# A list scheduler's priorities, a margin for transfers, and five tiles for rows of B, in a convolution, attention and selective-scan kernel

## The chip, the cores and the metric

The kernel runs on one core of one Trainium2 chip. A core has five engines with an instruction stream each: TensorE (PE, with its weight loads shown apart as PEld), VectorE (DVE), ScalarE (ACT), GpSimd (POOL) and SyncE (SP), which here issues the DMAs. The metric is the device time in microseconds; lower is better. All times are of fp32 work.

## The reference, cut to what matters

The input x has eight images of 56 x 56 tokens and 192 channels. Layer 0 adds to x an attention over a depthwise convolution of its group norm. Layer 1 adds a two-dimensional selective scan (SS2D), which is where most of the work lies:

```python
xz = einsum('bhwc,oc->bhwo', gn(x), in_proj_w)     # 192 -> 2 x 384
xa, z = split(xz)
xc = silu(depthwise_conv3x3(xa) + conv_b)
xs = [xc, xc transposed, and both reversed]         # 4 directions
dts, Bs, Cs = split(x_proj(xs))                     # 12, 16 and 16 rows
delta = softplus(dt_proj(dts) + bias)
for l in range(3136):                               # per direction
    h = exp(delta * A) * h + delta * B * u          # 384 channels x 16 states
    y[l] = sum over the 16 states of h * C
y = sum of the four directions (+ D * u)
out = x + out_proj(layernorm(y) * silu(z))
```

## The kernel before, in words

**Tiling.** A sequence of 3,136 tokens is cut into 7 chunks of T = 448 tokens. An image has 4 directions, so 28 chunks; the eight images have 224. Channels lie on the partitions, in 3 blocks j of 128. A chunk is scanned state by state, 16 states n, so there are 3,584 pairs (chunk i, state n). "Image" and "batch" mean the same below.

**Stages of the scan.** Each stage is a Python generator (lines 1044 to 1295):

- `prepared`: for each chunk, loads 12 delta rows (dts), C (ct_s) and the chunk of x (into du_s); PE projects the rows, and ACT and DVE make a softplus of them in the tile dl_s (L1066 to L1085, seven steps for each of three blocks); POOL then makes du_s = dl_s * x (L1089). dl_s and du_s have two tiles each.
- `row_loads`: for each state, broadcasts a row of B to 128 partitions (tile bb, 224 KB), and a row of C (cb) where POOL does the output.
- `inputs_made`: POOL makes h = du_s * bb, three blocks in one instruction (L1126). Tile h is taken from a ring of HBUFS tiles.
- `decays`: ACT makes da = exp(dl_s * A), a block at a time (L1140, two tiles).
- `scans`: DVE runs the recurrence in place in h (L1157). `carries`: DVE takes the last column as the start of the next chunk (newc, L1179).
- `turned`, `scaled`, `back`: PE transposes h (L1203, tile ht), ACT scales it by C (L1219, tile g), PE transposes it back and sums it over the states in PSUM (y, L1237; one y for the whole core).
- `by_pool`, `summed`: for 5 of the 16 states (3 in the last image), POOL multiplies h by C itself (L1256, L1260, tile yp) and PE adds the result to y (L1275).
- `skips` loads the chunk of x for the D term, and `evicted` adds y to the accumulator yacc on DVE (L1290, L1292).

Beside the scan of image b, `front` (group norms, convolutions, attention) and `x_proj` of image b + 1 are computed, and `finish` (layer norm, gate, output projection) of image b as its last direction ends.

**What sets the order.** None of this is written in the order in which it is issued. A list scheduler (class `Sched`) runs at build time. Every generator yields requests: an engine, an assumed cost, the cells that the step reads and those that it writes. `Sched.run` keeps a clock for each engine and takes, of all requests that can go, the one with the smallest t - rank, where t is the later of its inputs' and its engine's times. A rank of 0.4 thus lets a step be taken before another that could start up to 0.4 us sooner. The order found becomes the instruction order of each engine; on the chip the engines keep that order and wait on semaphores for the data. The ranks of the 13 scan stages are set where they are spawned (L1326): 0.30 for `prepared`, then 0.01 more for each, in the order `skips`, `row_loads`, `inputs_made`, `decays`, `scans`, `carries`, `turned`, `scaled`, `by_pool`, `back`, `summed`, `evicted` (0.42). `front` and `finish` have rank 0, and `URGENT` when they are behind their pace. For a DMA, the request has a fifth number: how long after its issue the data is assumed to be there.

```python
end = t + s.req[4] if len(s.req) > 4 else end + LATE[e]
```

Where the scheduler finds PE without work for over 0.45 us, it puts in fillers, matmuls of zeros (L1371)[...]. All DMAs go through SP's one queue, in the order found; a load that waits for its tile holds what stands behind it.

Of the kernel before, what the change touches and what calls it, by code (L numbers as in the profile page):

```python
# [21 lines left out]
T = 448  # L22
# [19 lines left out]
BY_POOL = (((2, 7), (12,)), ((2, 5), (8, 10), (13,)))  # L42
EPS = 1e-5
CAP = 60.0
HBUFS = 8
LEAD = 3


# [5 lines left out]
PE, ACT, DVE, POOL, SP = range(5)  # L54
LATE = (0.17, 0.08, 0.09, 0.06, 0.0)
HOP = 0.04
URGENT = 0.4


FILL = 64  # L60
# [103 lines left out]
class Sched:  # L164
# [37 lines left out]
    def give(self, s, t):  # L202

        e, cost, reads, writes = s.req[:4]
        end = t + cost
        self.at[e] = end
        self.used[e] += cost
        if s.group is not None and e == PE:
            self.spent[s.group] = self.spent.get(s.group, 0.0) + cost
        end = t + s.req[4] if len(s.req) > 4 else end + LATE[e]  # L210
        for c in reads:
            c.r = max(c.r, end)
        for c in writes:
            c.w = end
        s.end = max(s.end, end)
        self.resume(s)

    def run(self, until=None):
        while True:
# [20 lines left out]
            for s in self.stages:  # L240
# [3 lines left out]
                if s.group in self.limit:  # L244
# [4 lines left out]
                    if spent < must:  # L249
                        rank = URGENT  # L250
                e, _, reads, writes = s.req[:4]
# [21 lines left out]
def kernel(  # L273
# [93 lines left out]
    for nm, src in (("q", bn_q), ("kv", bn_kv)):  # L367
        p = load(f"bn{nm}", [CP, 4, NB], src.rearrange("v (b p) -> p v b", p=CP))
        s = const.tile([CP, NB], F32, name=f"bns{nm}")
        t = const.tile([CP, NB], F32, name=f"bnt{nm}")  # L370
# [30 lines left out]
    s3 = Rings(ctx.enter_context(tc.tile_pool(name="s3", bufs=3)), 3)  # L401
    sh = Rings(ctx.enter_context(tc.tile_pool(name="sh", bufs=HBUFS)), HBUFS)
    c1 = Rings(ctx.enter_context(tc.tile_pool(name="c1", bufs=1)), 1)
# [3 lines left out]
    sc = Sched()  # L407
# [57 lines left out]
    def dma(reads, writes, late, dst, src, after=()):  # L465
        yield SP, 0.07, reads, writes, late
        nc.sync.dma_start(dst, src)
        for t in after:
            t.free()
# [563 lines left out]
    for i in range(2):  # L1033
        t = keep.tile([128, T], F32, name=f"dts{i}")
# [70 lines left out]
    def row_loads():  # L1105
        for i, n in todo:
            b, k, c, _ = steps[i]
            yield lambda: i in chunks
            m = made[b]
            cols = slice(c * T, (c + 1) * T)  # L1110
            bb = yield s3("bb", [128, T])
            yield from dma([m["k_rows"][k, c]], bb.c, 3.2, bb.ap, m["rows"][k][R + n, cols].partition_broadcast(128))
            brow[i, n] = bb
            if n in by[i]:
                cbr = yield s2("cb", [128, T])
                yield from dma([m["k_rows"][k, c]], cbr.c, 3.2, cbr.ap,
                               m["rows"][k][R + NST + n, cols].partition_broadcast(128))
                crow[i, n] = cbr
# [178 lines left out]
    with tc.manual_schedule():  # L1297
        order = [(lay, c) for lay in range(2) for c in range(NCH)]

        with tc.tile_pool(name="p8", bufs=8, space=PSUM) as p8:  # L1300
            banks[0] = Ring(lambda: p8.tile([128, 512], F32, name="bank0"), 8)
            sc.spawn(front(0), 0.0, "front")
            sc.run()
            main = sc.spent.pop("front")
            sc.spawn(x_proj(0, order[:LEAD]), 0.0, "front")
            sc.run()
            each = sc.spent.pop("front") / LEAD

        with ExitStack() as es:
            py = es.enter_context(tc.tile_pool(name="py", bufs=1, space=PSUM))  # L1310
            pa = es.enter_context(tc.tile_pool(name="pa", bufs=2, space=PSUM))
            pb = [es.enter_context(tc.tile_pool(name=f"pb{i}", bufs=1, space=PSUM)) for i in range(3)]
            ybanks = py.tile([128, NJ, 512], F32, name="y")
            nc.vector.memset(ybanks, 0.0)
            ry = Ring(lambda: ybanks, 1)
            rda = Ring(lambda: pa.tile([128, 512], F32, name="da"), 2)
            three = [Tile(1) for _ in pb]

            def share(name, most):
                return Share(three, [lambda p=p: p.tile([128, 512], F32, name=name, tag="bank") for p in pb], most)  # L1320

            rht, rprep = share("ht", 2), share("prep", 1)
            banks[0] = share("bank1", 1)
            at["chunk"] = 0

            for rank, g in enumerate((prepared, skips, row_loads, inputs_made, decays, scans, carries, turned, scaled,  # L1326
                                      by_pool, back, summed, evicted)):
                sc.spawn(g(), 0.3 + 0.01 * rank, "scan")

            per = NDIR * NCH * NST  # L1330

            def ended(b):
                first = b * NDIR * NCH + (NDIR - 1) * NCH
                yield lambda: at["chunk"] >= first
                yield from finish(b, lambda c: lambda: at["chunk"] >= first + NCH - c, yread[b])

            def arounds():
                for b in range(nb):
                    yread[b] = {}
                    sc.spawn(ended(b), 0.0, "finish")  # L1340
                    if b > 0:
                        yield lambda: at["chunk"] >= b * NDIR * NCH
                    else:
                        yield from sc.join([sc.spawn(x_proj(0, order[LEAD:]), 0.0, "front")])
                    if b + 1 < nb:
                        yield from sc.join([sc.spawn(front(b + 1), 0.0, "front")])
                        yield from sc.join([sc.spawn(x_proj(b + 1, order), 0.0, "front")])

            def pace():

                b, slot = divmod(at["scan"], per)
                whole = main + len(order) * each
                lead = each * (len(order) - LEAD)
                before = b * whole + (lead if b else 0.0)
                here = whole + (0.0 if b else lead)
                late, share = (NDIR - 1) * NCH * NST, 0.87
                part = share * slot / late if slot < late else share + (1.0 - share) * (slot - late) / (per - 2 * NST - late)
                want = before + here * part
                return want + 12.0, want - 12.0

            def ending():
                done = sum(len(r) for r in yread.values())
                b, c = divmod(at["chunk"], NDIR * NCH)
                come = b * NCH + max(c - (NDIR - 1) * NCH, 0)
                return 1e9, 1e9 if done < come - 1 or done < b * NCH else 0.0

            def warm():

                while True:
                    yield PE, T_FILL, [], []  # L1370
                    nc.tensor.matmul(ybanks[:, 0, T:T + FILL], zeros, zeros[:, :FILL], start=False, stop=False)  # L1371

            def may():
                y = ys.get(at["y"])
                return y is not None and y["left"][0] > 0 and y["on"]

            at["y"] = -1
            filler = Stage(warm(), 0.0, 0.0, None)
            sc.resume(filler)
            sc.filler = filler, may  # L1380
            sc.limit["front"] = pace
            sc.limit["finish"] = ending
            sc.spawn(arounds(), 0.0)
            sc.run()
# [58 lines left out]
```

## Time and profile before

| | us |
|---|---|
| median of 3 runs (lowest, highest) | 18,865.54 (18,856.12, 18,895.47) |
| the profiled execution | 18,891.11 |
| its span, first to last instruction | 18,889.4 |
| busy: PE / DVE / ACT / POOL | 16,973.1 / 14,534.5 / 14,643.6 / 16,416.5 |
| granted TensorE clock, mean | 0.971 |
| DMA: share of 16 engines, rate | 32.2%, 93 GB/s |

The span covers all but 1.7 us of the profiled execution. Line numbers are those of the kernel before; in the changed kernel all lines after the constants are one higher. A group of instructions is shown as: line, engine, operation, tile written and tiles read, shapes, count, then busy us in all and mean ns of one, then the idle time of the engine just before them, with what ended most of it. The list of waits gives us in all, times, and the longest.

### The profile page before, as it was taken

To read this page: it belongs to the slowest core of one execution; us is meant where nothing else is said; L and a number is where in the kernel's file an instruction comes from. 1 tells how busy PE (TensorE), PEld (TensorE's weight loads), DVE (VectorE), ACT (ScalarE), POOL (GpSimd) and SP (SyncE) were. 2 spreads that over 40 slices of the span, in tenths; PEclk is the share of its full clock that TensorE was granted. 3 is DMA by queue.
4 is the path that set the end of the run, shared out by engine and by line. 5 is a ranking of instruction groups with operands and counts; after the bars stand their busy time and mean duration, and the time that the engine had idled before them with its cause. 6 is when DMAs were issued, how large, how long until landed. Compare 5 with 4: busy or idle time off the path is not lost. (4 is left out here: it accounts for less than half of the span.)

```text
span 18889.4 us, 274433 instructions
## 1 busy us (share of the span) xinstructions
PE 16973.1 (90%) x96640; PEld 11599.8 (61%) x96640; DVE 14534.5 (77%) x19156; ACT 14643.6 (78%) x26598; POOL 16416.5 (87%) x7528
## 2 busy tenths in 40 slices
PE   8789998999889998899898998889988899988888
PEld 4465566666666656665666655666556665666776
DVE  2387877887778777787777877778777788778887
ACT  2378877787777878778787887878778788888888
POOL 0388998899989999899998999989999899999997
PEclk9899999999999999999999999999999999999999
DMA  1332334323333333322333333332333333342222
GB/s 52 111 89 82 96 96 120 82 85 92 104 112 84 83 95 104 112 84 81 105 100 107 83 84 101 104 106 83 83 96 110 100 83 86 100 120 76 78 78 64
DMA packets 1128347, 1750.79 MB, mean 93 GB/s; under 512 B 168516, under 2 KB 1110840, under 8 KB 1123896
## 3 DMA queue, kind: packets, MB, share of 16 engines
q1 hardware_dynamic: 1126968, 1733.23, 32.2%
q8 instruction: 764, 12.52, 0.3%
q14 instruction: 615, 5.04, 0.1%
HBM read 1545.05 MB, written 187.74 MB: 92 GB/s over the span
## 5 line engine op out<-in xcount | busy, mean ns | idle before, releaser
L1157 DVE TENSOR_TENSOR_SCAN h<-da,newc,h 128x448 f32<-128x448 f32 x9216 | 10111.4, 1136 | 2166.1 <-ACT da L1140 1155.7
L1126 POOL TENSOR_TENSOR h<-du_s,bb 128x1344 f32<-128x1344 f32 x3584 | 10836.0, 3050 | 280.5 <-DMA bb<-rows 246.0
L1140 ACT ACTIVATE da<-dl_s,acoef 128x448 f32<-128x448 f32 x10752 | 6762.2, 636 | 1149.4 <-DVE h L1157 968.0
L1219 ACT ACTIVATE g<-ht,ct_s 112x384 f32<-112x384 f32 x10080 | 5663.7, 576 | 1776.0 <-PE ht L1203 1701.2
L1237 PE MATMUL y<-ident,g 112*128 112x112 f32 x30240 | 4742.3, 271 | 660.2 <-ACT g L1219 506.3
L1237 PEld LDWEIGHTS y<-ident,g 112*128 112x128 f32 x30240 | 3305.9, 143 | 3236.8 <-ACT g L1219 2466.3
L1203 PE MATMUL ht<-ident,h 128*112 128x128 f32 x30240 | 4935.7, 277 | 287.4 <-DVE h L1157 87.4
L1203 PEld LDWEIGHTS ht<-ident,h 128*112 128x112 f32 x30240 | 3481.3, 135 | 1064.4 <-issue 450.9
L1256 POOL TENSOR_TENSOR yp<-h,cb 128x448 f32<-128x448 f32 x1932 | 2147.0, 1143 | 454.8 <-PE y L1275 216.6
L1157 DVE TENSOR_TENSOR_SCAN h<-da,h 128x448 f32<-128x448 f32 x1536 | 1598.9, 1077 | 406.0 <-ACT da L1140 214.3
L1089 POOL TENSOR_TENSOR du_s<-dl_s,du_s 128x1344 f32<-128x1344 f32 x224 | 682.6, 3047 | 1338.5 <-DVE dl_s L1085 1300.8
L1256 POOL TENSOR_TENSOR h<-h,cb 128x448 f32<-128x448 f32 x1260 | 1399.1, 1141 | 291.3 <-issue 175.6
L1371 PE MATMUL y<-zeros 128*128 128x64 f32 x11944 | 1651.3, 272 | 0.0
L1371 PEld LDWEIGHTS y<-zeros 128*128 128x128 f32 x11944 | 1586.1, 198 | 48.6 <-issue 48.6
L1275 PE MATMUL y<-yp,ident 128*128 128x448 f32 x3864 | 1594.0, 547 | 5.1 <-POOL yp L1260 4.5
L453 PE MATMUL bank<-xa,dg 128*128 128x440 f32 (+2 forms) x3024 | 1318.4, 543 | 89.0 <-ACT g L1219 52.2
L1260 POOL TENSOR_TENSOR yp<-yp,h 128x1344 f32<-128x1344 f32 x420 | 1280.9, 3050 | 1.6
L757 PE MATMUL bank<-qT,kT 128*112 128x448 f32 x2352 | 1101.8, 559 | 83.8 <-ACT pT L707 47.2
L766 PE MATMUL bank<-pT,vt 112*128 112x448 f32 x2352 | 1002.1, 546 | 66.8 <-ACT pT L707 43.4
L1275 PEld LDWEIGHTS y<-yp,ident 128*128 128x128 f32 x3864 | 701.3, 193 | 551.6 <-issue 505.2
L453 PE MATMUL bank<-band,dgq 96*96 96x440 f32 (+3 forms) x2016 | 860.9, 544 | 54.4 <-ACT hq L583 29.9
L707 ACT ACTIVATE pT<-bank,nsh 112x448 f32<-112x448 f32 x1176 | 744.3, 635 | 172.9 <-PE bank L757 152.5
(152 smaller groups left out, 12958.1 us busy)
## 6 DMA issues: line engine op xcount, KB each, us to landing
bb<-rows SPq DMA_DIRECT2D x3584, 224.0 KB
cb<-rows SPq DMA_DIRECT2D x1064, 224.0 KB
xt<-x1d SPq DMA_DIRECT2D x224, 336.0 KB
du_s<-xch SPq DMA_DIRECT2D x112, 672.0 KB
du_s<-xcw SPq DMA_DIRECT2D x112, 672.0 KB
xch<-xv SPq DMA_DIRECT2D x24, 1568.0 KB
xcw<-xw SPq DMA_DIRECT2D x168, 224.0 KB
xs<-xch SPq DMA_DIRECT2D x56, 672.0 KB
```

The lines of the kernel that those rows point to most:

```text
L453: nc.tensor.matmul(out[:, o0:o1, a:b], lhs, img(lo, hi)[:, :, a + dx - 1:b + dx - 1], start=(t == TAPS[0]), stop=(t == TAPS[-1]))
L757: nc.tensor.matmul(ps.ap[:TP, :T], kts[h][:, kb * TP:(kb + 1) * TP], qh.ap, start=True, stop=True)
L1126: nc.gpsimd.tensor_tensor(h.ap, du.ap, bb.ap.unsqueeze(1).to_broadcast([128, NJ, T]), ALU.mult)
L1140: nc.scalar.activation(da.ap[:, :T], dl.ap[:, j], AF.Exp, scale=acoef[:, k * NJ + j, n:n + 1])
L1157: nc.vector.tensor_tensor_scan(h.ap[:, j, rev], da.ap[:, 0:T][:, rev], h.ap[:, j, rev], news[i - 1].ap[:, j, n:n + 1] if ci else 0.0, ALU. ...
L1203: nc.tensor.transpose(ht.ap[:TP, j * 128:(j + 1) * 128], h.ap[:, j, s * TP:(s + 1) * TP], ident)
L1219: nc.scalar.activation(g.ap, ht.ap[:TP, :DIN], AF.Copy, scale=ct.ap[:, s, n:n + 1])
L1237: nc.tensor.matmul(y["t"].ap[:, j, s * TP:(s + 1) * TP], g.ap[:, j * 128:(j + 1) * 128], ident[:TP, :TP], is_transpose=True, start=(n == 0 ...
L1256: nc.gpsimd.tensor_tensor(to.ap[:, j], h.ap[:, j], cbr.ap, ALU.mult)
L1260: nc.gpsimd.tensor_tensor(yp.ap, yp.ap, h.ap, ALU.add)
L1275: nc.tensor.matmul(y["t"].ap[:, j, :T], ident, yp.ap[:, j], start=False, stop=(y["left"][j] == 0))
L1371: nc.tensor.matmul(ybanks[:, 0, T:T + FILL], zeros, zeros[:, :FILL], start=False, stop=False)
```

## The change

It sets constants and ranks; no step of the computation is added or taken out.

- A DMA's data is assumed to be there `MARGIN` = 3 us later than before.
- `URGENT` goes from 0.4 to 0.9.
- Rows of B (bb) have five tiles instead of three; h has seven instead of eight. In bytes per partition of SBUF: 2 x 1,792 more, 5,376 less.
- The 13 stages get a rank each, by name.

```diff
-HBUFS = 8
+HBUFS = 7
...
-URGENT = 0.4
+MARGIN = 3.0
+URGENT = 0.9
...
-        end = t + s.req[4] if len(s.req) > 4 else end + LATE[e]
+        end = t + s.req[4] + MARGIN if len(s.req) > 4 else end + LATE[e]
...
-            bb = yield s3("bb", [128, T])
+            bb = yield s3("bb", [128, T], 5)
...
-            for rank, g in enumerate((prepared, skips, row_loads, inputs_made, decays, scans, carries, turned, scaled,
-                                      by_pool, back, summed, evicted)):
-                sc.spawn(g(), 0.3 + 0.01 * rank, "scan")
+            for g, rank in ((prepared, 0.3), (skips, 0.0), (row_loads, 0.25), (inputs_made, 0.0), (decays, 0.37),
+                            (scans, 0.16), (carries, 0.36), (turned, 0.37), (scaled, 0.38), (by_pool, 0.39),
+                            (back, 0.4), (summed, 0.0), (evicted, 0.71)):
+                sc.spawn(g(), rank, "scan")
```

## The prediction

> **What bounds the kernel now.** I read the page's busy shares first: five engines, none full, POOL the fullest of those with work of their own.
>
> ```profile
> PE 16973.1 (90%) x96640; PEld 11599.8 (61%) x96640; DVE 14534.5 (77%) x19156; ACT 14643.6 (78%) x26598; POOL 16416.5 (87%) x7528
> ```
>
> PE's 90% includes fillers. The costliest groups show how much, and what POOL does:
>
> ```profile
> L1126 POOL TENSOR_TENSOR h<-du_s,bb 128x1344 f32<-128x1344 f32 x3584 | 10836.0, 3050 | 280.5 <-DMA bb<-rows 246.0
> ...
> L1256 POOL TENSOR_TENSOR yp<-h,cb 128x448 f32<-128x448 f32 x1932 | 2147.0, 1143 | 454.8 <-PE y L1275 216.6
> ...
> L1089 POOL TENSOR_TENSOR du_s<-dl_s,du_s 128x1344 f32<-128x1344 f32 x224 | 682.6, 3047 | 1338.5 <-DVE dl_s L1085 1300.8
> L1256 POOL TENSOR_TENSOR h<-h,cb 128x448 f32<-128x448 f32 x1260 | 1399.1, 1141 | 291.3 <-issue 175.6
> L1371 PE MATMUL y<-zeros 128*128 128x64 f32 x11944 | 1651.3, 272 | 0.0
> ```
>
> Fillers (L1371) are 1651 us, so PE's own work is 15,322 us, under POOL's 16,416. POOL starts at 783.6 us (the first du_s) and could not end before 783.6 + 16,416 = 17,200 us. It loses 18,889.4 - 17,200 = 1,690 us: the last column gives du_s 1,338 less the start, L1126 280, L1256 455 + 291. POOL's list of waits separates the start:
>
> ```profile
> POOL du_s L1089 <- DVE dl_s L1085: 1300.8, 78, 729.9
> POOL h L1126 <- DMA bb<-rows: 246.0, 74, 9.7
> POOL yp L1256 <- PE y L1275: 216.6, 55, 12.9
> ...
> POOL h L1256 <- DVE newc L1179: 93.0, 36, 10.1
> ...
> POOL du_s L1089 <- DVE newc L1179: 37.4, 13, 6.4
> ```
>
> 729.9 us is the prologue, so du_s waits 1,338.5 - 729.9 = 609 us in the scan, always at the seam of two chunks. The timeline of POOL and of DVE at one seam:
>
> ```profile
> 8031.45 3.05 POOL L1126 TENSOR_TENSOR h<-du_s,bb 128x1344 f32<-128x1344 f32 x1
> 8041.89 3.04 POOL L1089 TENSOR_TENSOR du_s<-dl_s,du_s 128x1344 f32<-128x1344 f32 x1 [7.39 <-DVE dl_s L1085]
> 8045.01 12.06 POOL L1126 TENSOR_TENSOR h<-du_s,bb 128x1344 f32<-128x1344 f32 x4
> ...
> 8041.20 0.61 DVE L1085 TENSOR_TENSOR dl_s<-prep,dl_s 128x448 f32<-128x448 f32 x1
> 8041.73 0.61 DVE L595 TENSOR_REDUCE qm<-qe 128x1 f32<-128x448 f32 x1
> 8048.09 3.48 DVE L1157 TENSOR_TENSOR_SCAN h<-da,newc,h 128x448 f32<-128x448 f32 x3 [5.75 <-POOL h L1126]
> ```
>
> The delta of the new chunk (dl_s) is finished at 8,041.8 us; POOL has stood 7.39 us, makes du_s, then the first h, and DVE has stood 5.75 us when its scan starts. Taking the start of every state's first scan from the trace, over the seven batches with front work a state follows the last one after 4.74 us on average inside a chunk and after 9.38 us at a seam. The seam is not idle everywhere: PE is busy there with its own work 8.64 of the 9.38 us. Last, the batches, cut at their first scans (columns: busy us of PE, PEld, DVE, ACT, POOL):
>
> ```profile
> 7679.00:9980.00 2301.00, 2088.13 (x11792) 1414.47 (x11790) 1810.38 (x2386) 1815.64 (x3296) 2085.67 (x965) 0.97 0.33 96
> ...
> 16875.00:18889.00 2014.00, 1763.72 (x12360) 1400.34 (x12359) 1701.65 (x2186) 1738.70 (x3225) 1812.60 (x763) 0.96 0.27 78
> ```
>
> In a batch with front work PE (fillers in) and POOL are both busy 2,086 to 2,088 of 2,301 us. That pair is what limits the gain.
>
> **What the Trainium skill says.** "Perfetto Trace Analysis", Tensor Engine Instruction: ACT, DVE and GpSimd are strict first-in first-out. The trace agrees: nothing of POOL's passes the du_s that stands 7.39 us. "GPSIMD Engine Reference", 2.1 Instruction dispatch: a two-input body has a floor near 2.5 cycles per element; at its 1.2 GHz an estimate of 2.8 us for 1,344 elements, beside 3.05 us measured, so order can't shorten POOL's work, only its waits. "DMA: Bandwidth & Descriptors", Anatomy of one DMA: about 2.0 us fixed plus bytes / 436 GB/s (for GpSimd's path), and waits are held by the issuing sequencer. An estimate of 2.5 us for a 224 KB row of B; in this trace the product starts 3.8 us after the issue at the earliest, 9.4 us in the median.
>
> **The change part by part.** The programs of both kernels have the same instructions on DVE (19,158), ACT, POOL and SP (7,013, so no DMA more or less); PE has 340 fillers more (5,972 to 6,312). All else is order.
>
> *Delta earlier (ranks of prepared, scans, inputs_made).* Before, stage prepared (0.30) stood under scans (0.35) and inputs_made (0.33); now it stands over both (0.16 and 0). In the order of the built programs, du_s came after all 16 products of the chunk before in each of 224 chunks; now it comes 5.1 states earlier on average (2 at least). On DVE the last dl_s moves from 1.6 states ahead of its chunk's first scan to 7.6. Its loads move too: the 12 delta rows (dts) are issued on SP 18 rows of B ahead of the chunk's own instead of 16, its xs rows 9 instead of 10; both still lie ahead of need. So the 609 us of du_s waits should fall to some 40: -569. Ends: 0 if dl_s is late again, -609.
>
> *Rows of B (five tiles, MARGIN).* A tile's next load waits on SP for the product that frees it; with three tiles there are two products, about 9.4 us, between issue and use, with five four. Behind a waiting row on SP stand stores and loads of the front, which gain likewise. 246 us of waits to some 60: -186. Ends: 0, -246. MARGIN puts every user of a transfer 3 us later in the order; on the chip it waits only if the order has nothing else for it.
>
> *POOL's shares of y (by_pool, summed).* L1256 waits 746 us. In the orders POOL has made 2.2 states beyond the one it multiplies before, 2.9 after, so scan and carry are done more often when POOL comes to it; against it, summed falls from 0.41 to 0, which frees yp later (216.6 us of the 746). I take a third off, -250; ends +200, -500.
>
> *Seven h tiles.* L1126 waits 280 us in all, 246 for rows of B; so at most 35 us for a free h with eight. Taken as nothing, since products lie only 0.2 to 6.8 us ahead of their scans on average (hidden by that slack); up to +100 if POOL, no longer stopped at seams, runs into the seventh tile.
>
> *Urgent front (0.4 to 0.9), back, evicted.* Front work that is behind its pace now goes ahead of everything. PE's runs of front matmuls between scan matmuls grow longer: 288 of over 3 us instead of 113 (at 0.81 us per 448 columns, from three of L1275 in 2.42 us). The work is the same; ACT waits for ht longer in a run and less elsewhere. Zero, ends -100 and +790 (below).
>
> *Fillers.* 340 x (1,651.3 / 5,972 = 0.277 us) = 94 us on PE, 289 of them in the last batch, where PE has 2,014 - 1,764 = 250 us idle. Hidden; +94 if not.
>
> Sum on POOL: -569 - 186 - 250 = -1,005 us, or 125 us a batch. That would put a 2,297 us batch at 2,172 with PE and POOL both at 96%. Two in-order engines that wait for each other don't both get there; I give back 40% (waits of PE on g, of POOL on h) and take -600: batches near 2,222, both engines at 94%. 18,889 - 600 = 18,289 us for the profiled span. That execution took 18,891.1 us, the median of the runs is 18,865.5, so x 0.9986: 18,265 us.
>
> **Rivals.**
> (a) *PE is the wall.* For: at the seam PE was busy 8.64 of 9.38 us, and in batches 1 to 6 the fillers stay at 664 to 673 each (664 to 674 before), so the order leaves PE as much to wait as ever. Against: fillers aren't work, and PE idles 213 us a batch besides. Then two thirds of the gain of seams and rows go (755 / 3 = 250): about 18,600.
> (b) *Nothing is given back*: all 1,005 us: about 17,860. For: POOL's lead is larger everywhere. Against: both engines at 96%.
> (c) *Front bursts starve the scan*, slower. Place: PE, where ht and y stand behind a run of front matmuls, ACT waits for ht (1,701 us already), h tiles stay taken, with one fewer. Price: 175 more runs of some 4.5 us, 790 us if each stops the scan for its length: 18,865 - 600 + 790 = 19,055. It decides from 600 / 175 = 3.4 us lost in each. Against: POOL and DVE have slack of up to 6.8 us, and the total of front work is unchanged.
> (d) *The seam only moves*: delta is early but decays or y's single bank (evicted) hold the first scan: no change, 18,865.
>
> **How the numbers follow.** Forecast 0.60 (18,000 to 18,500), (a) 0.17, (b) 0.12, (c) 0.08, (d) 0.03. The range runs from (b) to the upper part of (a): 17,850 to 18,780, leaving out some 0.06 below and 0.13 above. Faster by over 0.2% (38 us, about what a measurement here tells from none) 0.88: forecast, (b) and nearly all of (a); within 0.2% 0.03; slower 0.09.
>
> **What would show it.** Right: L1089's wait under 770 us in all with the prologue, L1126's for bb under 100, seams near 5.5 us, POOL at 89 to 91% of the span, batches near 2,222. Wrong: seams as before, or ACT's wait for ht and PE's for g up by hundreds of us; a new POOL wait on h behind PE ht would point to the seventh tile; a last batch longer than 2,014 us to the fillers.

## The result, and the profile after

The changed kernel takes 18,645.61 us (median of 4 runs, 18,636.89 to 18,648.41), beside 18,874.99 us for the kernel before. The ratio is 0.9874, 95% interval 0.986 to 0.9888: faster by 1.3%, or 229 us. The forecast was 18,265 us, 3.2% faster. The time lies in the stated range, and the direction was right, but the gain is less than half of what was forecast.

The groups that the prediction was built on, in the page of the changed kernel (idle time before the group stands last):

```profile
L1127 POOL TENSOR_TENSOR h<-du_s,bb 128x1344 f32<-128x1344 f32 x3584 | 10816.3, 3051 | 272.1 <-PE ht L1204 185.5
...
L1257 POOL TENSOR_TENSOR yp<-h,cb 128x448 f32<-128x448 f32 x1932 | 2147.1, 1142 | 371.8 <-PE y L1276 213.2
...
L1257 POOL TENSOR_TENSOR h<-h,cb 128x448 f32<-128x448 f32 x1260 | 1399.6, 1141 | 530.5 <-DVE newc L1180 265.8
...
L1372 PE MATMUL y<-zeros 128*128 128x64 f32 x12624 | 1708.4, 273 | 0.0
L1090 POOL TENSOR_TENSOR du_s<-dl_s,du_s 128x1344 f32<-128x1344 f32 x224 | 682.3, 3046 | 906.0 <-DVE dl_s L1086 839.4
```

POOL's list of waits after (us in all, times, longest):

```profile
POOL du_s L1090 <- DVE dl_s L1086: 839.4, 64, 727.5
POOL h L1257 <- DVE newc L1180: 265.8, 124, 13.7
...
POOL yp L1257 <- PE y L1276: 213.2, 96, 11.2
POOL h L1127 <- PE ht L1204: 185.5, 60, 9.1
POOL h L1127 <- DMA bb<-rows: 66.6, 25, 5.2
```

The two waits that were to go did go. Without the prologue's 727.5 us, du_s waits 906.0 - 727.5 = 179 us instead of 609, and the product waits 67 us for rows of B instead of 246. Two others grew: the multiplications by C (L1257) wait 371.8 + 530.5 = 902 us instead of 746, and the product waits 186 us for a free h (behind PE ht), which the list of waits before did not show among its longest. In sum POOL's idle time after its first du_s fell by some 260 us, about what the kernel gained.

At a seam, POOL now makes du_s in the midst of its products (timeline of POOL, about where the seam of the prediction stood):

```profile
8006.35 3.04 POOL L1261 TENSOR_TENSOR yp<-yp,h 128x1344 f32<-128x1344 f32 x1
8009.56 3.04 POOL L1090 TENSOR_TENSOR du_s<-dl_s,du_s 128x1344 f32<-128x1344 f32 x1 [0.17 <-DVE dl_s L1086]
8012.57 6.05 POOL L1127 TENSOR_TENSOR h<-du_s,bb 128x1344 f32<-128x1344 f32 x2
```

Over the seven batches with front work, the first scan of a chunk follows the last state's after 4.80 us instead of 9.38, so the seam is gone. But from state to state inside a chunk it is 5.09 us instead of 4.84 (the 4.74 of the prediction is the mean of all eight batches; that of the seven is 4.84). Fifteen intervals longer by 0.25 us take 3.8 of the 4.6 us back that the seam gave, and 0.8 us a chunk are left.

PE shows where the rest went. Its own work (fillers left out, counted in the trace) was 8.64 us in a seam and 4.05 us in an interval inside a chunk; after, it is 4.35 and 4.32 us. While POOL and DVE stood in a seam, PE was doing work of the front and of the scan's last states. That work has moved, and each of the fifteen intervals carries 0.27 us more of it. The last image, without front work, loses in the same way (4.23 us inside a chunk instead of 4.02), but its seam falls further, from 9.81 to 3.83 us, so 2.8 us a chunk are left. Its rows, before and after (span of the stretch, then busy us of PE, PEld, DVE, ACT and POOL):

```profile
16874.80:18889.00 2014.20, 1763.92 (x12362) 1400.44 (x12359) 1701.85 (x2187) 1738.70 (x3225) 1812.80 (x763) 0.96 0.27 78
```

```profile
16707.20:18641.00 1933.80, 1764.67 (x12888) 1411.34 (x12886) 1726.26 (x2183) 1723.54 (x3219) 1815.84 (x764) 0.99 0.28 80
```

80 us of the gain come from this one image; the six images in the middle gain 164 us together (13,801 to 13,637), the first gains nothing. The experiments ask how much of what was taken back belongs to the moved seam, and how much to the other parts of the change.

### The profile page after: what moved, and what is told of

The parts are those of the page before. It is cut to its first block, busy times and chain, and to the rows that moved or that the text cites. A ratio compares the mean times of both kernels' runs of the same rounds, so it can differ in the third digit from the quotient of the medians.

```text
span 18641.6 us, 275449 instructions
## 1 busy us (share of the span) xinstructions
PE 16947.4 (91%) x97320; PEld 11601.9 (62%) x97320; DVE 14715.5 (79%) x19156; ACT 14638.2 (79%) x26598; POOL 16430.8 (88%) x7528
## 5 line engine op out<-in xcount | busy, mean ns | idle before, releaser
L1220 ACT ACTIVATE g<-ht,ct_s 112x384 f32<-112x384 f32 x10080 | 5529.3, 575 | 1119.8 <-PE ht L1204 974.5
L1238 PE MATMUL y<-ident,g 112*128 112x112 f32 x30240 | 4586.8, 270 | 523.8 <-ACT g L1220 353.7
L1204 PE MATMUL ht<-ident,h 128*112 128x128 f32 x30240 | 4709.0, 275 | 160.7 <-DVE oT L721 68.1
L1257 POOL TENSOR_TENSOR yp<-h,cb 128x448 f32<-128x448 f32 x1932 | 2147.1, 1142 | 371.8 <-PE y L1276 213.2
L1257 POOL TENSOR_TENSOR h<-h,cb 128x448 f32<-128x448 f32 x1260 | 1399.6, 1141 | 530.5 <-DVE newc L1180 265.8
L1276 PE MATMUL y<-yp,ident 128*128 128x448 f32 x3864 | 1750.2, 545 | 8.0 <-POOL yp L1257 4.7
L1372 PEld LDWEIGHTS y<-zeros 128*128 128x128 f32 x12624 | 1655.6, 198 | 86.7 <-issue 86.7
L1372 PE MATMUL y<-zeros 128*128 128x64 f32 x12624 | 1708.4, 273 | 0.0
L1090 POOL TENSOR_TENSOR du_s<-dl_s,du_s 128x1344 f32<-128x1344 f32 x224 | 682.3, 3046 | 906.0 <-DVE dl_s L1086 839.4
L454 PE MATMUL bank<-xa,dg 128*128 128x440 f32 (+2 forms) x3024 | 1263.1, 535 | 45.2 <-ACT g L1220 21.2
L1067 PE MATMUL prep<-dts,dtw 128*128 128x448 f32 x1344 | 662.4, 575 | 143.5 <-DVE dl_s L1086 130.4
```

Source lines behind the costliest of these rows:

```text
L454: nc.tensor.matmul(out[:, o0:o1, a:b], lhs, img(lo, hi)[:, :, a + dx - 1:b + dx - 1], start=(t == TAPS[0]), stop=(t == TAPS[-1]))
L1204: nc.tensor.transpose(ht.ap[:TP, j * 128:(j + 1) * 128], h.ap[:, j, s * TP:(s + 1) * TP], ident)
L1220: nc.scalar.activation(g.ap, ht.ap[:TP, :DIN], AF.Copy, scale=ct.ap[:, s, n:n + 1])
L1238: nc.tensor.matmul(y["t"].ap[:, j, s * TP:(s + 1) * TP], g.ap[:, j * 128:(j + 1) * 128], ident[:TP, :TP], is_transpose=True, start=(n == 0 ...
L1257: nc.gpsimd.tensor_tensor(to.ap[:, j], h.ap[:, j], cbr.ap, ALU.mult)
L1276: nc.tensor.matmul(y["t"].ap[:, j, :T], ident, yp.ap[:, j], start=False, stop=(y["left"][j] == 0))
```

## The experiments

Every kernel computes the whole reference; e7 and e8 add work that is not needed. Ratios are to the kernel before on the same chip, with their 95% intervals.

| kernel | ranks | URGENT | MARGIN | h / bb tiles | us | ratio |
|---|---|---|---|---|---|---|
| before | old | 0.4 | 0 | 8 / 3 | 18,875 | 1 |
| after | new | 0.9 | 3 | 7 / 5 | 18,646 | 0.9874 (0.986 to 0.9888) |
| e1 | new | 0.4 | 0 | 8 / 3 | 18,454 | 0.9772 (0.9756 to 0.9789) |
| e2 | old | 0.4 | 0 | 7 / 5 | 18,831 | 0.9974 (0.9965 to 0.9983) |
| e3 | new | 0.9 | 0 | 7 / 5 | 18,703 | 0.9906 (0.9889 to 0.9923) |
| e4 | new | 0.4 | 3 | 7 / 5 | 18,547 | 0.9821 (0.9804 to 0.9838) |
| e5 | new | 0.9 | 0 | 8 / 3 | 18,787 | 0.9952 (0.9935 to 0.9968) |
| e6 | new | 0.4 | 0 | 7 / 3 | 18,472 | 0.9785 (0.977 to 0.9799) |
| e9 | old | 0.9 | 0 | 8 / 3 | 19,414 | 1.0286 (1.0271 to 1.0301) |
| e10 | two new | 0.4 | 0 | 8 / 3 | 18,501 | 0.9802 (0.9785 to 0.9818) |
| e11 | new | 0.4 | 0 | 7 / 5 | 18,499 | 0.9803 (0.9789 to 0.9818) |
| e12 | new | 0.4 | 3 | 8 / 3 | 18,509 | 0.9808 (0.9794 to 0.9823) |

### One part at a time (e1 to e4)

Theory 1: the ranks end the seam's wait, and what eats the rest is the nearness of PE and POOL. Theory 2: the transfers are the gain. e1 is the new ranks alone:

```diff
-            for rank, g in enumerate((prepared, skips, row_loads, inputs_made, decays, scans, carries, turned, scaled,
-                                      by_pool, back, summed, evicted)):
-                sc.spawn(g(), 0.3 + 0.01 * rank, "scan")
+            for g, rank in ((prepared, 0.3), (skips, 0.0), (row_loads, 0.25), (inputs_made, 0.0), (decays, 0.37),
+                            (scans, 0.16), (carries, 0.36), (turned, 0.37), (scaled, 0.38), (by_pool, 0.39),
+                            (back, 0.4), (summed, 0.0), (evicted, 0.71)):
+                sc.spawn(g(), rank, "scan")
```

> The kernel before with the 13 new ranks alone (URGENT 0.4, no MARGIN, three bb, eight h). Theory 1 (the ranks end the wait at the seams, and PE with POOL as near neighbour limits what that is worth): du_s waits fall by 350 to 450 us in the scan, the time by 120 to 220 us, to about 18,700. Theory 2 (the gain is that of the transfers, MARGIN and five tiles; ranks only move the seam's wait elsewhere): under 50 us, 18,830 to 18,900.

Measured: 18,454.13 us, faster than either theory had it, and 191 us faster than the whole change. URGENT, MARGIN and the tiles together take 191 us of the ranks' gain back. Most of the longer intervals, though, come with the ranks: in e1 an interval inside a chunk takes 5.03 us (4.84 before, 5.09 in the changed kernel), with 0.22 us more of PE's own work in it, and a seam 4.86. So 2.7 of the 4.5 us that the seam gives go back with URGENT at 0.4 too.

e2 is the tiles alone:

```diff
-HBUFS = 8
+HBUFS = 7
-            bb = yield s3("bb", [128, T])
+            bb = yield s3("bb", [128, T], 5)
```

> The kernel before with five bb and seven h tiles alone. Theory 1: waits for rows of B fall from 246 us to under 100, the seams stay, the time falls by 30 to 80 us (18,800 to 18,845). Theory 2: 130 us or more. If the seventh h tile costs something by itself: no gain or slower.

Measured: 18,830.66 us, 46 us faster; waits for rows of B 84 us instead of 246, du_s waits as before. Theory 1 holds for this part. Five bb tiles beside eight h tiles were not run.

e3 takes MARGIN out of the changed kernel, e4 puts URGENT back:

```diff
-MARGIN = 3.0
+MARGIN = 0.0
```

> The changed kernel with MARGIN 0. Theory 1: waits for transfers come back in part (up to 100 us), the time is 18,650 to 18,750. Theory 2 (the transfers are the gain): 18,780 or more.

```diff
-URGENT = 0.9
+URGENT = 0.4
```

> The changed kernel with URGENT back at 0.4, so that front work that is late no longer goes ahead of every scan stage. If long runs of front matmuls keep the scan waiting (the slower rival in small): runs over 3 us fall back and the time falls by 50 to 200 us, to 18,450 to 18,600. If they are neutral: within 30 us of the changed kernel's 18,646.

Measured: 18,703.28 us for e3, so MARGIN is worth 57 us in this company. But not through the waits that theory 1 named: those for rows of B are 47 us in e3, less than the 67 of the changed kernel. What grew is L1257, from 902 to 965 us. 18,546.51 us for e4: URGENT 0.9 costs 99 us in the changed kernel. That is the part which the prediction had priced at zero. The multiplications by C don't show it; they wait 536 + 368 = 904 us in e4, as in the changed kernel:

```profile
L1257 POOL TENSOR_TENSOR yp<-h,cb 128x448 f32<-128x448 f32 x1932 | 2149.9, 1145 | 535.9 <-PE y L1276 410.8
L1257 POOL TENSOR_TENSOR h<-h,cb 128x448 f32<-128x448 f32 x1260 | 1405.3, 1146 | 368.3 <-DVE newc L1180 288.4
```

### URGENT, the seventh tile, and the walls (e5 to e8)

e5 is e1 with `URGENT = 0.9`; e6 is e1 with `HBUFS = 7`.

> The kernel with the new ranks alone (18,454 us) and URGENT 0.9 beside them; no MARGIN, three bb, eight h. If URGENT is what gives the ranks' gain back: 18,530 to 18,600, with ACT's wait for ht and POOL's waits at L1256 up. If it is the tiles and the seventh h tile instead: within 30 us of 18,454.

> The kernel with the new ranks alone and seven h tiles instead of eight; three bb. If the seventh tile costs (POOL's wait for a free h, behind PE ht): 18,510 to 18,560, with that wait above 100 us. If eight were more than enough: within 30 us of 18,454.

Measured: e5 18,787.33 us, 333 us more than e1 and worse than expected; e6 18,472.14 us, its interval overlapping that of e1, so the seventh h tile costs nothing that can be told. Its wait is real (154 us for PE ht), but is hidden.

e5 is the clearest picture of the case. Its du_s waits less than in any other kernel: 780.1 us with a prologue of 728.8, so 51 us in the whole scan. Yet its six middle batches take 13,789 us, the kernel before 13,801. The stretch of those batches, in e1 and then in e5:

```profile
3020.40:16517.90 13497.50, 12388.23 (x70584) 8433.88 (x70582) 10953.34 (x14307) 10865.54 (x19778) 12524.02 (x5785) 0.98 0.34 98
```

```profile
3052.30:16841.30 13789.00, 12474.46 (x70560) 8487.49 (x70560) 11079.26 (x14306) 10905.93 (x19778) 12517.07 (x5785) 0.97 0.34 96
```

POOL does the same work in both; it stands 1,272 us in e5 and 973 us in e1. Where it stands in e1 and in e5 (its waits without the prologue's line):

```profile
POOL yp L1256 <- PE y L1275: 356.1, 98, 33.2
POOL h L1126 <- DMA bb<-rows: 192.2, 79, 7.6
POOL h L1256 <- DVE newc L1179: 169.8, 61, 8.7
```

```profile
POOL yp L1256 <- PE y L1275: 433.3, 141, 14.2
POOL h L1256 <- DVE newc L1179: 371.1, 72, 17.7
POOL h L1126 <- DMA bb<-rows: 233.2, 85, 15.6
POOL h L1256 <- issue: 195.1, 75, 8.2
```

POOL waits less for delta and more for newc, the carry of the state that it is to multiply by C: scan and carry of that state come later. The next links are in the list of waits of all engines, again e1 and then e5:

```profile
DVE h L1157 <- ACT da L1140: 1178.6, 1550, 8.5
...
ACT pT L707 <- PE bank L757: 110.3, 154, 15.8
```

```profile
DVE h L1157 <- ACT da L1140: 1401.1, 1799, 8.5
...
ACT pT L707 <- PE bank L757: 350.6, 251, 28.6
```

ACT stands at the attention's exponentials (pT), which wait for their scores; decays stand behind it in ACT's queue, and scans wait longer for da. This made ACT the first suspect. TensorE's granted clock can be set aside: it is 0.976 in e1 and 0.971 in e5, and PE is busy only 86 us longer in these batches with as many matmuls (12,388 and 12,474 us).

e7 and e8 put work on one engine of the changed kernel behind the scheduler's back, to see which engine is a wall. e7, behind a state's last transposes (and only while y is open), 2,438 in all:

```diff
+                if s == SUB - 1 and i in ys and ys[i]["on"] and ys[i]["left"][0] > 0:
+                    nc.tensor.matmul(ybanks[:, 0, T:T + FILL], zeros, zeros[:, :FILL], start=False, stop=False)
```

e8, behind the product of each state that PE sums, on a tile of its own:

```diff
+            if n not in by[i]:
+                nc.gpsimd.tensor_tensor(spare, spare, spare, ALU.mult)
```

> The changed kernel with one filler more on PE (2,438 in all) after a state's last transposes, which the scheduler does not know of: 2,438 x 0.277 = 675 us of PE work. If PE is the wall: 450 us or more later (19,100 and up). If PE has room beside the scan: under 250 us (below 18,900). The output is that of the reference.

> The changed kernel with one small product more on POOL (128x32 on a tile of its own) for the 2,520 states that PE sums, which the scheduler does not know of: by the lengths of its 448 and 1,344 wide products about 0.26 us each, 655 us. If POOL is the wall: 450 us or more later. If PE is the wall and POOL has room: under 250 us (below 18,900).

Measured: e7 18,729.96 us, 84 us more, and e8 18,828.97 us, 183 us more. By the lengths of one instruction the added work is 675 us on PE and 2,520 x 0.250 = 630 us on POOL, so 12% and 29% of it reach the end. The busy times of the changed kernel, e7 and e8 say less was added:

```profile
PE 16947.4 (91%) x97320; PEld 11601.9 (62%) x97320; DVE 14715.5 (79%) x19156; ACT 14638.2 (79%) x26598; POOL 16430.8 (88%) x7528
```

```profile
PE 17243.0 (92%) x102196; PEld 12158.8 (65%) x102196; DVE 14726.9 (79%) x19156; ACT 14661.6 (78%) x26598; POOL 16439.3 (88%) x7528
```

```profile
PE 17004.5 (90%) x97320; PEld 11637.8 (62%) x97320; DVE 14756.9 (78%) x19156; ACT 14651.6 (78%) x26598; POOL 16922.7 (90%) x10049
```

PE's busy time grew by 296 us and POOL's by 492, since the records of neighbouring instructions overlap in the trace. Against these, 28% and 37% reach the end. Either way most of it is hidden: at the places where the work was added, neither engine is a wall. The rival "PE is the wall" had named nearly the right time (18,600), and theory 1 agreed in its second half; e7 speaks against both as they stand. It does not test PE's work at other places. Whether PE's work that left the seams makes the intervals longer, or another link in the engines' waits for each other does, stays open.

### URGENT alone, two ranks alone, and the other corners (e9 to e12)

e9 is the kernel before with `URGENT = 0.9`. e10 lowers two ranks only:

```diff
-                sc.spawn(g(), 0.3 + 0.01 * rank, "scan")
+                sc.spawn(g(), {scans: 0.16, inputs_made: 0.0}.get(g, 0.3 + 0.01 * rank), "scan")
```

e11 is e1 with the tiles, e12 is e1 with 3.0 us added to a transfer's time.

> The kernel before with URGENT 0.9 alone. If urgent front work costs by itself, wherever the ranks stand (it cost 333 us beside the new ranks): 19,000 to 19,250, with ACT's idle time before front steps well above its 383 us. If it costs only beside the new ranks: within 60 us of 18,880.

> The kernel before with two ranks alone: scans 0.16 and inputs_made 0, so that the next chunk's delta goes ahead of both. If the gain of the ranks is that of the seams: 18,450 to 18,600, du_s waits in the scan under 200 us instead of 609. If it needs the other ranks (carries, evicted, summed): over 18,700.

> The new ranks with five bb and seven h tiles, URGENT 0.4, no MARGIN. Waits for rows of B below 80 us instead of 192. If MARGIN is what makes the kernel with all but URGENT (18,546) slower than the ranks alone (18,454): 18,400 to 18,460. If it is the tiles: 18,520 or more.

> The new ranks with MARGIN 3, URGENT 0.4, three bb, eight h. It has some 570 fillers more than the ranks alone. If MARGIN costs beside URGENT 0.4: 18,500 to 18,580. If it is neutral or helps, as beside URGENT 0.9 (57 us faster): 18,380 to 18,460.

Measured: e9 19,414.22 us, 535 us slower than before: dearer than expected, and not a matter of the new ranks. e10 18,500.58 us: two ranks bring 378 of the 422 us that all thirteen bring, and du_s waits 911.3 - 727.4 = 184 us in the scan. So most of the ranks' gain comes with the two that close the seam. e11 18,498.58 us, between the two ranges that were expected, and e12 18,508.96 us: beside URGENT 0.4 neither the tiles nor MARGIN help; MARGIN costs 55 us, and the tiles some 44, with intervals that just touch. Beside URGENT 0.9 both helped (84 and 57 us). What one part is worth depends on the others that stand beside it.

### How URGENT costs (e13 to e18)

There were two readings: long runs of front matmuls on PE (the slower rival), or ACT standing at front steps. A late front step is a step of `front` or `finish` that is behind its pace. e13 to e15 are e1 with the rank 0.9 for late front steps of one engine alone, e16 is e1 with `URGENT = 0.6`.

```diff
-                        rank = URGENT
+                        rank = 0.9 if s.req[0] == PE else URGENT
```

> The new ranks alone, with rank 0.9 for late front steps of PE only (0.4 on the other engines). If runs of front matmuls ahead of the scan are the cost: most of the 333 us, 18,650 to 18,790. If the cost is ACT standing at front steps: under 100 us, below 18,550.

> The new ranks alone, with rank 0.9 for late front steps of ACT only. If ACT standing at front steps is the cost: most of the 333 us, 18,650 to 18,790, with ACT's idle time before front steps near 800 us. If it is PE's runs: below 18,550.

> The new ranks alone, with rank 0.9 for late front steps of DVE only. DVE's idle time before front steps grew less (452 to 568 us), so both readings expect under 100 us, below 18,550.

> The new ranks alone, URGENT 0.6. A cost that grows with the lead that a late front step may take gives some 18,550 to 18,650, between 18,454 (0.4) and 18,787 (0.9). A threshold at the ranks of the scan (0.36 to 0.40 for most) would put it near 18,787 already.

Measured:

| kernel | 0.9 for | us | against e1 |
|---|---|---|---|
| e1 | none | 18,454 | |
| e5 | all | 18,787 | +333 |
| e13 | PE | 18,666 | +212 |
| e14 | ACT | 18,337 | -117 |
| e15 | DVE | 18,719 | +265 |
| e16 | all, 0.6 | 18,502 | +48 |

The suspicion of ACT falls: with ACT alone at 0.9 the kernel is the fastest of all, ratio 0.9712 (0.9697 to 0.9726), though pT waits 245 us there too. Long runs fall as well. Counted in the traces of the seven batches with front work (front matmuls one after another, no scan matmul or filler between, over 3 us from the first start to the last end), e1 has 230 of them, e13 only 185, and e13 is 212 us slower. DVE, expected to be harmless, costs most. The three engines sum to +360 us, about the 333 of all together; the front's loads on SP were not tried alone. e16 came out below both of its ranges: the cost neither grows evenly with the lead nor is there at once.

What was left is what a rank does in the rule t - rank. Where inputs are there, t is the same for all and 0.4 already goes ahead of nearly all scan stages, so 0.9 changes little. Where a front step's input is expected late, 0.9 lets it take an engine's place up to 0.5 us earlier than 0.4 does, and on DVE 0.74 us earlier than a scan (rank 0.16). The engine then stands for it, though a scan step may be ready behind. e17 and e18 part the two (hurry is true for a late front step; e18 has > in place of <=):

```diff
+                    if hurry and t + HOP <= self.at[e]:
+                        rank = 0.9
                     t = max(t + HOP, self.at[e])
```

> The new ranks alone; a late front step has rank 0.9 if its input is there when its engine is free, else 0.4. If keeping the place for a step whose input is late is the cost: within 60 us of 18,454. If passing ready scan steps is the cost: 18,700 or more.

> The new ranks alone; a late front step has rank 0.9 if its input comes only after its engine is free, else 0.4. If keeping the place is the cost: 18,700 to 18,850, most of the 333 us, and PE's idle time before front steps near 780 us instead of 568. If passing ready steps is the cost: within 60 us of 18,454.

Measured: e17 18,507.58 us, ratio 0.9807 (0.9792 to 0.9822), 53 us more than e1; e18 18,701.94 us, ratio 0.9907 (0.989 to 0.9923), 248 us more. Keeping a place for a late input is most of the cost. The idle time of PE just before front steps, summed over the seven batches with front work, goes the same way: 568 us in e1, 658 in e17, 782 in e18, 787 in e5.

The granted clock is no rival here: it was 0.974 to 0.975 in the runs of e17 and 0.974 to 0.976 in those of e18.

So it is shown, beside the new ranks and over all engines together, that places kept for late inputs cost. Why ACT's places, kept in the same way, gain instead is not settled. Nor was it measured how far the time moves when the order is changed for no reason. The differences of some 50 us between two orders (e11, e12, e16, e17) lie at the edge of the noise of the runs, and no mechanism is shown for them.

## Why the prediction was wrong

**The sum from before to after**, from runs that differ in one part: ranks -422 (to e1), URGENT +333 (to e5), tiles -84 (to e3), MARGIN -57 (to the changed kernel): -230 us, the measured 229. It has to come out, whatever the order in which parts are added; the shares don't. By way of e1, e11 and e4 they are ranks -422, tiles +44, MARGIN +48, URGENT +99. Common to both are -422 for the ranks and +191 for the other three. The prediction had, after its give-back of 40%, 0.6 x (569 + 250) = 491 us of gain for the ranks and 0.6 x 186 = 112 for the rest. So some 300 of the 371 us that are missing lie in URGENT, tiles and MARGIN together.

**The step that failed is "Urgent front (0.4 to 0.9): Zero".** It measured +99 us in the changed kernel (e4), +333 beside the new ranks and +535 alone. The prediction saw front work move ahead of the scan and held it to be neutral because the work stays the same, with the cost of long runs as a rival at 0.08. The cost is real, but beside the new ranks it isn't that of runs (nor did ACT's wait for ht, the place that this rival named, grow in the changed kernel: it fell from 1,701 to 975 us). Beside the new ranks most of it (248 us, e18) lies in places kept for inputs that come late. That split was not made in the changed kernel. The rule points there: where inputs are ready, going from 0.4 to 0.9 can hardly change which step is taken.

**Delta earlier: right.** The forecast of -569 us in du_s's waits measured -430 in the changed kernel and -557 in e5. In time the two ranks brought 378 us (e10), beside 425 us of du_s waits removed; POOL's other waits moved as well. What the prediction left out is that PE's work in the seams, which it had counted (8.64 of 9.38 us), goes into the intervals inside the chunks. Two of the signs that it named for being right failed too: L1090 waits 906 us with the prologue, not under 770, and POOL is busy 88% of the span, not 89 to 91.

**Rows of B: right as a wait** (-186 forecast, 246 to 67 measured), and too high as time: the tiles brought 46 us alone (e2), for 162 us of waits removed, and beside the new ranks and URGENT 0.4 nothing (e11). That the sum adds this term to that of the ranks is the second step that failed.

**POOL's shares of y: wrong in sign.** Forecast -250, measured +156. Its argument was the distance in the order: 2.9 states made ahead instead of 2.2. With the ranks alone the fall isn't there either: 464.5 + 302.5 = 767 us in e1, beside 746 before. URGENT is not the cause in the changed kernel (904 us in e4), though it adds 364 us in e5. Neither the tiles nor MARGIN alone bring it beside the ranks (774 us in e11, 708 in e12), so what makes it 902 stays open. Distance in one engine's order says nothing on when another engine gets there.

**Seven h tiles: zero was right in time** (e6 not to be told from e1), though the wait it named appeared (186 us in the changed kernel).

**Fillers: nothing speaks against zero.** 12 to 28% of e7's fillers reach the end, which would make some 11 to 26 us of 94; that is an estimate, as e7's stand at other places.

**The give-back of 40%: neither shown nor refuted.** It put batches at 2,222 us, with PE and POOL at 94%. The changed kernel takes 13,637 us for six, 2,273 each. e14 runs its six middle batches in 13,367 us, 2,228 each, with POOL busy 94% and PE 92%, so such batches can be had. But e14 is another kernel, and what a us of POOL's waits was worth in time differs from part to part (0.9 in e10, 0.3 in e2). A forecast of 2,222 met there is luck as far as the 40% go:

```profile
3025.40:16392.00 13366.60, 12318.92 (x69858) 8322.47 (x69857) 10994.12 (x14307) 10879.92 (x19779) 12521.57 (x5785) 0.98 0.35 99
```

e14 is the fastest kernel of the case: the new ranks, eight h and three bb tiles, no MARGIN, URGENT 0.4 but 0.9 for ACT's front steps, 18,337.26 us, 2.9% under the kernel before and 1.7% under the changed one (18,337 / 18,646).

## What to carry to other kernels

In a list scheduler that takes the smallest t - rank, a priority is also a permission to keep an engine waiting: the difference of two ranks is the time for which a ready step may stand behind one that isn't ready. Raise it with care, engine by engine (here it cost on PE and DVE and gained on ACT), and look for its cost in the idle time before the steps that it favours and in the waits of those they displace. Before counting a gap as a gain, ask what other engines do in it: that work has to go somewhere. When a change sets several constants together, run each alone, and the whole without each: here the ranks were worth 422 us, URGENT cost 99 to 535 us by what stood beside it, and MARGIN changed its sign with it.

## What was not expected

An engine that is busy 91% of the span can have slack for most of what is added to it at one place: fillers priced at 675 us on PE cost 84 us, and small products priced at 630 us on POOL (88% busy) cost 183 us. Where engines wait for each other, their busy shares don't tell the bound; work added on one of them tells more, for the place where it is added.
